# A planner's product given to either of two engines, with corrected durations: a Mamba-and-MLP block on one core

## The chip, the cores and the metric

The kernel runs on one core of a Trainium2 chip. The time is device microseconds of one execution; the figure compared is the median of several. The core's engines are TensorE (PE, matmuls, written into PSUM), VectorE (DVE), ScalarE (ACT), GpSimd (POOL) and SyncE (SP, which here issues nearly all DMAs). Each engine runs its own instructions in the order in which the program lists them, and waits at semaphores for what another engine must finish first.

## The reference, cut to what matters

The input x has 8 images of 384 channels by 1024 positions, in float32. Each image passes through a state-space ("Mamba") block with an MLP behind it and a residual; images 0 to 4 then pass through a feed-forward layer with signed weights and quantised activations.

```python
t = (t - mu) * rsqrt(var + 1e-05) * ln_w + ln_b          # norm over channels
xm, z = split(t @ in_proj_w.T, 2)                        # 768 inner channels each
xc = silu(causal_conv(xm, conv_w) + conv_b)              # 3 taps
dt, Bm, Cm = split(xc @ x_proj_w.T, [24, 40])
dt = softplus(dt @ dt_proj_w.T + dt_proj_b)
dA  = exp(dt * A)                                        # 16 states per channel
dBu = (dt * xc) * Bm
h_t = dA_t * h_(t-1) + dBu_t;  y_t = sum_n(h_t * C_t)    # scan over 1024 positions
t = ((y + xc * D) * silu(z)) @ out_proj_w.T
t = gelu(t @ mlp_w1.T + mlp_b1) @ mlp_w2.T + mlp_b2      # x = x + t
# images 0 to 4: t = t + bitlinear(gelu(bitlinear(norm(t), W1)), W2)
```

The product `dt * xc` is the one that the change's name speaks of.

## The kernel before, in words

**Stages.** Per image b there are four pieces of work. `s1` does the norm, the two input projections (PSUM tiles `p_in` and `p_z`), the convolution, the low-rank projections (`p_dbc`, `p_all`, `p_dt`), Softplus, and the product `dtx = xc * dt`. It works on two halves of 512 positions; each half has three products, each over 128 partitions by 2 x 512 elements (L817), so 48 in all. A product is written with its two inputs interleaved and then stored to DRAM (L518). `s2` is the scan: 12 units per image, 96 in all, each with four quads of states. In a unit POOL multiplies `dtx_r` by a row of B (tile `u`, L965), ACT makes `da` by Exp (L557), DVE runs the recurrences (L990), POOL or DVE multiplies by a row of C (L965, or L1010 and L1012), and PE adds the 16 states up with a folding matrix into the PSUM tile `py` (L929). `s3` does the output projection and the MLP (`p_out`, `p_h`, `p_o`, all at L541). `ffn` does the feed-forward layer (`p_y1` and `p_y2`, also L541). Most matmuls go through one helper (L541), most ACT instructions through another (L557), and evictions of PSUM through `affine` (L570 and L572 on ACT, L577 and L579 on DVE or POOL).

**The norm.** `norm` (from L590) is called 26 times. It adds three slices of 512 into `total`, in two POOL additions (L628, L629) or in one DVE reduction (L632); it takes the mean with one matmul (`p_mean`, L640), subtracts it on DVE (L643), squares on ACT, sums the squares with 12 small matmuls (`p_var`, L599), turns the result (`p_turned`, L654), adds eps (DVE, L658), raises to -0.5 (POOL, L660), spreads it with four matmuls (`p_r`, L617) and multiplies (DVE, L664).

**The planner.** No instruction stands where the Python code would put it. All operations are first written down with `add(engine, cost, emit, r=..., w=...)`: the engine, an assumed duration in us, what it reads and writes. `Plan.run` (L248) then plays them through a clock of its own: it repeatedly takes the engine that can start something first and chooses among what is ready, by rank; the scan comes before the other work. The order in which it emits is each engine's order in the program. An assumed duration therefore does not change what an instruction costs; it changes what the planner believes to be ready, and so the order of everything behind it.

Two rules of the planner matter here. The first is for operations that have a second engine (`others`). They belong to the first engine, and another may take one as a guest if it can start it at least `HOST` = 0.3 us before the first engine comes free, and would be done with it before it could start anything of its own (L329):

```python
if s + HOST < free[op.engine] and (
    first is None or s + op.others[e][0] <= first
) and (best is None or s < best[0]):
```

The second is for gaps on PE. Where the planner sees PE without work for more than `IDLE` = 0.7 us and a PSUM buffer free, it puts in `spare` matmuls of 128x256 (L451), which compute nothing that is used, one after the other until the gap is down to 0.7 us (L347). The number of `spare` matmuls in a program thus says how much standing still the planner foresaw on PE. In the profile a float32 matmul counts as two instructions.

Tiles come from rings of a few buffers; the product's output shares the ring `sq` (two buffers) with the norm's `total` and `sq`. All PSUM tiles other than `py` and `da` share the ring `mm` of three buffers, the `spare` ones too.

Of the kernel before, what the change touches and what calls it, by code (L numbers as in the profile page):

```python
# [35 lines left out]
KC = C // P  # L36
# [7 lines left out]
PER = 2  # L44
T = 512
# [26 lines left out]
MM = 0.859  # L72
# [19 lines left out]
def c_act(n):  # L92
    return 0.2 + n * 0.00084


def c_dve(n):
    return 0.17 + n * 0.00102
# [90 lines left out]
class Plan:  # L188
# [12 lines left out]
    def add(self, engine, cost, emit, r=(), w=(), claim=(), table=None, size=0, others=None,  # L201
            land=1.6, rate=350e3, lag=None, tiled=False):
        op = Op()
        op.engine, op.cost, op.emit, op.table = engine, cost, emit, table
        op.others, op.settle = others or {}, None
        op.size, op.land, op.prio = 0.03 + size / rate, land - 0.1, (*self.prio, len(self.ops))
        op.next, op.ready, op.tiles, op.tiled = [], 0.0, [], tiled
        op.lag = LAG.get(engine, 0.0) if lag is None else lag
        op.slack = SLACK if self.prio[0] < 0 else 0.0
        deps = set()  # L210

        def parts_of(t):
            t, part = t if isinstance(t, tuple) else (t, None)
            if t not in op.tiles:
                op.tiles.append(t)
                if t.ring is not None:
                    t.left += 1
            if part is None:
                if None not in t.parts:
                    t.parts[None] = [None, []]  # L220
                return list(t.parts.values())
            if part not in t.parts:
                whole = t.parts.get(None)
                t.parts[part] = [whole[0], list(whole[1])] if whole else [None, []]
            return [t.parts[part]]

        for t in claim:
            t.left += 1
            op.tiles.append(t)
        for t in r:  # L230
            for p in parts_of(t):
                if p[0] is not None:
                    deps.add(p[0])
                p[1].append(op)
        for t in w:
            for p in parts_of(t):
                if p[0] is not None:
                    deps.add(p[0])
                deps.update(p[1])
                p[0], p[1] = op, []  # L240
        deps.discard(op)
        op.wants = len(deps)
        for d in deps:
            d.next.append(op)
        self.ops.append(op)
        return op
# [144 lines left out]
class Layer:  # L391
# [198 lines left out]
    def norm(self, t, eps, scale):  # L590

        nc, add = self.nc, self.plan.add
        def columns(src, name):
            p = self.piece("mm", [P, TG], name)

            def emit():
                for k in range(KC):
                    for g in range(G):
                        nc.tensor.matmul(  # L599
                            p.real[g * DQ : (g + 1) * DQ, :], self.ones[:, :DQ],  # L600
                            src.real[:, k, g * TG : (g + 1) * TG],
                            start=(k == 0), stop=(k == KC - 1),
                        )

            add("PE", 0.79, emit, r=[src], w=[p], tiled=True)
            return p

        def spread(src, name, turned=False):
            p = self.piece("mm", [P, T], name)

            def emit():
                for g in range(G):
                    if turned:
                        by, of = src.real[:, g : g + 1], self.ident
                    else:
                        by, of = self.ident[:, g * DQ : g * DQ + 1], src.real
                    nc.tensor.matmul(  # L617
                        p.real[:, g * TG : (g + 1) * TG], by.to_broadcast([P, P]), of,
                        start=True, stop=True,
                    )  # L620

            add("PE", 0.89, emit, r=[src], w=[p])
            return p

        total = self.piece("sq", [P, T], "total")

        def in_two():
            nc.gpsimd.tensor_add(total.real, t.real[:, 0, :], t.real[:, 1, :])  # L628
            nc.gpsimd.tensor_add(total.real, total.real, t.real[:, 2, :])  # L629

        def at_once():
            nc.vector.tensor_reduce(  # L632
                total.real, t.real.rearrange("p k l -> p l k"), AX.X, ALU.add
            )

        add("POOL", 2.5, in_two, r=[t], w=[total], others={
            "DVE": (c_dve(KC * T) + 0.02, at_once)
        })
        p_mean = self.piece("mm", [P, T], "p_mean")
        add("PE", MM, lambda: nc.tensor.matmul(  # L640
            p_mean.real, self.ones, total.real, start=True, stop=True
        ), r=[total], w=[p_mean])
        add("DVE", c_dve(KC * T) + 0.05, lambda: nc.vector.scalar_tensor_tensor(  # L643
            t.real, p_mean.real.unsqueeze(1).to_broadcast([P, KC, T]), -1.0 / C, t.real,
            ALU.mult, ALU.add,
        ), r=[p_mean], w=[t])

        sq = self.piece("sq", [P, KC, T], "sq")
        self.act(lambda: sq.real, lambda: t.real, AF.Square, c_act(KC * T), r=[t], w=[sq])
        p_var = columns(sq, "p_var")  # L650
        var = self.piece("rstd", [P, TG], "var")
        self.affine(lambda: var.real, lambda: p_var.real, [p_var], [var], scale=scale, n=TG)
        p_turned = self.piece("mm", [P, G], "p_turned")
        add("PE", 0.14, lambda: nc.tensor.matmul(  # L654
            p_turned.real, var.real, self.ident[:, ::DQ], start=True, stop=True
        ), r=[var], w=[p_turned])
        rstd = self.piece("root", [P, G], "rstd")
        add("DVE", 0.15, lambda: nc.vector.tensor_scalar_add(rstd.real, p_turned.real, eps),  # L658
            r=[p_turned], w=[rstd])
        add("POOL", 1.0, lambda: nc.gpsimd.tensor_tensor(  # L660
            rstd.real, rstd.real, self.power.to_broadcast([P, G]), ALU.pow
        ), w=[rstd])
        p_r = spread(rstd, "p_r", True)
        add("DVE", c_dve(KC * T), lambda: nc.vector.tensor_mul(  # L664
            t.real, t.real, p_r.real.unsqueeze(1).to_broadcast([P, KC, T])
        ), r=[p_r], w=[t])
# [3 lines left out]
    def s1(self, b):  # L670
        nc, a, add = self.nc, self.a, self.plan.add
# [21 lines left out]
        def normed(half):  # L693
            t = self.piece(r_t, [P, KC, T], "t")
            src = a["x"][b][:, HALVES[half]].rearrange("(k p) l -> p k l", p=P)
            with self.plan.lane(14 if b == 1 else 4):
                self.load(t, lambda x: x, src, size=4 * P * KC * T)
                self.norm(t, E1 * E2, (1.0 + E2) / C)
                for k in range(KC):
                    self.affine(  # L700
                        lambda k=k: t.real[:, k, :], lambda k=k: t.real[:, k, :], [], [t[k]],
                        self.ln_b[:, k : k + 1], self.ln_w[:, k : k + 1], pool=True,
                    )
            return t
# [11 lines left out]
        for half, cols in enumerate(HALVES):  # L716
            t = normed(half)


            xc = self.split(r_x, KD, "xc")  # L720
            for m in range(KD):
                w = self.weights(r_w, KC, a["in_proj_w"][m])
# [42 lines left out]
            w = self.weights(r_w, KC, a["x_proj_w"])  # L765
# [23 lines left out]
            dt = self.split(r_x, KD, "dt")  # L789
            for k in range(0, KD, 2):  # L790
                if k % KC != 2:
                    w = self.weights(r_w, KC, a["dt_proj_w"][k // KC])
                else:
                    w, before = self.weights(r_w, KC, a["dt_proj_w"][1]), w
# [3 lines left out]
                def two(k=k, pds=pds, dbc=dbc, ws=ws):  # L798
# [8 lines left out]
                    tiled=True)  # L807
# [6 lines left out]
            d = self.dram["dtx", b]  # L814
            for p in range(KC):
                dtx = self.piece("sq", [P, T, 2], "dtx")
                add("POOL", 2.35, lambda p=p, dtx=dtx, xc=xc, dt=dt: nc.gpsimd.tensor_mul(  # L817
                    dtx.real.rearrange("p n i -> p i n"), xc.pieces[p].real, dt.pieces[p].real
                ), r=[xc[2 * p], xc[2 * p + 1], dt[2 * p], dt[2 * p + 1]], w=[dtx])
                self.store(d.real[p, :, half * L : (half + 1) * L], dtx,  # L820
                           lambda x: x.rearrange("p n i -> p (n i)"), [d[p, half]], 4 * P * L)
            d = self.dram["dt", b]
# [582 lines left out]
```

## Time and profile before

| what | value |
|---|---|
| median of 6 runs | 3201.33 us (3197.01 to 3203.86) |
| the profiled execution | 3203.86 us, of which the span from first to last instruction is 3202.0 us |
| mean granted TensorE clock | 0.987 of full speed |
| DMA | 751.78 MB, 234 GB/s of HBM traffic over the span |
| p_h, p_o, p_y1 and p_y2 matmuls (L541), busy together | 515.6 + 510.5 + 322.1 + 323.6 us |
| POOL's multiplies of the scan (L965) | 1186.3 + 900.6 + 397.1 us |
| DVE's recurrences (L990) | 870.0 + 382.0 + 281.8 us and smaller groups |

How to read it: "busy" is the time in which an engine works on an instruction; the span is the time from the first to the last instruction of the core. In the rows of groups, a line, an engine, an operation and its tiles are followed by the count, the busy time, the mean ns of one, and then the time for which the engine stood idle just before these instructions, with what ended the idle time. Tiles have the program's names without their numbers. A row of waits names who waited for whom, with the total, the number of times and the longest. Durations come from this one execution.

### The profile page before, as it was taken

To read this page: it belongs to the slowest core of one execution; us is meant where nothing else is said; L and a number is where in the kernel's file an instruction comes from. 1 tells how busy PE (TensorE), PEld (TensorE's weight loads), DVE (VectorE), ACT (ScalarE), POOL (GpSimd) and SP (SyncE) were. 2 spreads that over 40 slices of the span, in tenths; PEclk is the share of its full clock that TensorE was granted. 3 is DMA by queue.
4 is the path that set the end of the run, shared out by engine and by line. 5 is a ranking of instruction groups with operands and counts; after the bars stand their busy time and mean duration, and the time that the engine had idled before them with its cause. 6 is when DMAs were issued, how large, how long until landed. Compare 5 with 4: busy or idle time off the path is not lost.

```text
span 3202.0 us, 32487 instructions
## 1 busy us (share of the span) xinstructions
PE 3087.2 (96%) x10286; PEld 1263.8 (39%) x10286; DVE 2602.3 (81%) x2058; ACT 2020.9 (63%) x2397; POOL 2805.3 (88%) x1097
## 2 busy tenths in 40 slices
PE   9898999998999999999999999999999999999999
PEld 4333433343433443434344334343434443333333
DVE  4787887889977798798898888997788977888881
ACT  4878786767665565665675576457566565655662
POOL 2879978989989898999989999899989999998990
PEclk9899999999999999999999999999999999999999
DMA  7889878767777667766586686777767756755542
GB/s 239 295 294 302 268 233 301 258 214 246 252 277 247 206 197 247 277 224 228 197 301 243 212 299 216 250 229 271 244 222 268 243 184 215 230 183 184 170 153 72
DMA packets 348970, 751.78 MB, mean 235 GB/s; under 512 B 36480, under 2 KB 113792, under 8 KB 339584
## 3 DMA queue, kind: packets, MB, share of 16 engines
q1 hardware_dynamic: 348368, 749.61, 69.6%
q8 instruction: 83, 1.36, 0.2%
q14 instruction: 87, 0.71, 0.1%
q10 hardware_dynamic: 432, 0.09, 0.0%
HBM read 569.21 MB, written 180.36 MB: 234 GB/s over the span
## 4 chain that ended last, share of the span: by engine, by line
PE 69%; DVE 10%; DMA 8%; ACT 6%; POOL 4%; issue 3%; SPq 1%; DVEq 0%; POOLq 0%; ACTq 0%
PE p_y L541 16%; PE p_h L541 12%; PE p_o L541 11%; PE py L929 8%; PE p_z L541 6%; PE p_in L541 6%; PE p_out L541 5%; DVE da L990 3%; DVE u L990 3%; POOL u L965 3%; ACT da L557 2%; DMA dtx_r<-dtx_d 2%; ACT L557 1%; DMA dt_r<-dt_d 1%; DMA w_b<-in_mlp_w 1%
## 5 line engine op out<-in xcount | busy, mean ns | idle before, releaser
L965 POOL TENSOR_TENSOR u<-dtx_r,bc 128x2048 f32<-128x2048 f32 (+1 forms) x360 | 1186.3, 3312 | 93.6 <-PE py L929 55.0
L557 ACT ACTIVATE da<-dt_r,a_neg 128x1024 f32<-128x1024 f32 (+1 forms) x960 | 898.7, 944 | 579.1 <-DVE u L990 312.1
L965 POOL TENSOR_TENSOR u<-u,bc 128x2048 f32<-128x2048 f32 (+1 forms) x274 | 900.6, 3293 | 134.9 <-DVE u L990 122.4
L990 DVE TENSOR_TENSOR_SCAN u<-da,u 128x1024 f32<-128x1024 f32 (+1 forms) x436 | 870.0, 2007 | 155.8 <-ACT da L557 80.3
L541 PE MATMUL p_h<-t,w_b 128*128 128x512 f32 x1152 | 515.6, 600 | 15.5 <-DMA w_b<-in_mlp_w 10.2
L541 PE MATMUL p_o<-g,w 128*128 128x512 f32 x1152 | 510.5, 596 | 6.2 <-DMA w<-in_mlp_w 2.7
L990 DVE TENSOR_TENSOR_SCAN da<-da,dtx_r 128x1024 f32<-128x1024 f32 (+1 forms) x192 | 382.0, 2015 | 64.6 <-POOL dtx_r L965 43.1
L965 POOL TENSOR_TENSOR dtx_r<-dtx_r,bc 128x2048 f32<-128x2048 f32 (+1 forms) x120 | 397.1, 3314 | 1.9
L541 PEld LDWEIGHTS p_h<-t,w_b 128*128 128x128 f32 x1152 | 215.0, 191 | 307.1 <-issue 260.1
L541 PEld LDWEIGHTS p_o<-g,w 128*128 128x128 f32 x1152 | 215.1, 190 | 295.7 <-issue 279.6
L541 PE MATMUL p_y<-gf,w_n 128*128 128x512 f32 x720 | 323.6, 602 | 6.2 <-ACT dt L572 3.7
L541 PE MATMUL p_y<-tn,w_b 128*128 128x512 f32 x720 | 322.1, 602 | 6.3 <-DVE tn L664 3.5
L929 PE MATMUL py<-u,fold 128*32 128x512 f32 x2304 | 305.7, 629 | 5.9 <-POOL u L965 5.9
L990 DVE TENSOR_TENSOR_SCAN da<-da,u 128x1024 f32<-128x1024 f32 (+1 forms) x140 | 281.8, 2038 | 33.9 <-ACT da L557 18.4
L557 ACT ACT_TABLE_LOAD x211 | 270.7, 1283 | 6.5 <-DMA dt_r<-dt_d 2.8
L541 PE MATMUL p_out<-yg,w 128*128 128x512 f32 x552 | 244.9, 595 | 4.9 <-DMA w<-in_out_proj_w 2.2
L541 PE MATMUL p_in<-t,w_f 128*128 128x512 f32 x504 | 232.2, 609 | 17.4 <-ACT t L572 4.7
L541 PE MATMUL p_z<-t,w_f 128*128 128x512 f32 x504 | 233.1, 610 | 9.7 <-DMA w_f<-in_in_proj_w 8.1
L541 PEld LDWEIGHTS p_y<-gf,w_n 128*128 128x128 f32 x720 | 134.9, 191 | 190.9 <-issue 171.9
L541 PEld LDWEIGHTS p_y<-tn,w_b 128*128 128x128 f32 x720 | 135.2, 191 | 189.0 <-issue 168.6
L572 ACT ACTIVATE y<-p_y,v_vecs 128x512 f32<-128x512 f32 x145 | 98.8, 682 | 134.1 <-PE p_y L541 109.0
L572 ACT ACTIVATE g<-p_h,v_vecs 128x512 f32<-128x512 f32 x159 | 108.0, 680 | 115.4 <-PE p_h L541 114.7
(132 smaller groups left out, 3266.6 us busy)
## 6 DMA issues: line engine op xcount, KB each, us to landing
dtx_r<-dtx_d SPq DMA_DIRECT2D x72, 1024.0 KB, 5.8
dt_r<-dt_d SPq DMA_DIRECT2D x144, 512.0 KB, 5.0
w_b<-in_mlp_w SPq DMA_DIRECT2D x192, 192.0 KB, 3.3
w<-in_mlp_w SPq DMA_DIRECT2D x96, 384.0 KB, 3.3
w_f<-in_in_proj_w SPq DMA_DIRECT2D x168, 192.0 KB, 4.3
y_d<-y SPq DMA_DIRECT2D x120, 256.0 KB, 4.9
gf<-y_d SPq DMA_DIRECT2D x60, 512.0 KB, 6.7
xc_d<-xc SPq DMA_DIRECT2D x48, 512.0 KB, 6.5
```

The costliest lines, as they stand in the source:

```text
L541: self.nc.tensor.matmul(p.real, w.real[:, w0 + k, :], t.at(k0 + k), start=start and k == 0, stop=stop and k == n - 1,)
L557: lambda: self.nc.scalar.activation(out(), in_(), func, **{k: v() if callable(v) else v for k, v in kw.items()}),
L572: nc.scalar.activation(out(), in_(), AF.Identity, bias=bias, scale=scale)
L929: nc.tensor.matmul(py.real[g * DQ : (g + 1) * DQ, :], self.fold, hc, start=False, stop=(q == NQUAD - 1), skip_group_check=True,)
L965: nc.gpsimd.tensor_mul(u.real[:, x], t.real[:, x], row.real.unsqueeze(2).to_broadcast([P, n, 2]))
L990: da=da, in_u=in_u: nc.vector.tensor_tensor_scan(to(i), da.real[:, i, :], in_u(i), state.real[:, col : col + 1] if half else 0.0, ALU.mult ...
```

## The change

Four assumed durations of the norm are replaced: the 12 `p_var` matmuls 0.79 to 0.68 us, the four `p_r` matmuls 0.89 to 0.98, the `p_mean` matmul 0.859 to 0.939, the two POOL additions 2.5 to 2.64 and their single DVE form 1.757 to 1.91. The product `dtx`, so far on POOL alone, gets DVE as its second engine, with an assumed duration of 0.17 + 1024 x 0.00102 = 1.21 us; on POOL it keeps its 2.35. What is computed stays the same. Lines behind L817 move down by six.

```diff
-            add("PE", 0.79, emit, r=[src], w=[p], tiled=True)
+            add("PE", 0.68, emit, r=[src], w=[p], tiled=True)
...
-            add("PE", 0.89, emit, r=[src], w=[p])
+            add("PE", 0.98, emit, r=[src], w=[p])
...
-        add("POOL", 2.5, in_two, r=[t], w=[total], others={
-            "DVE": (c_dve(KC * T) + 0.02, at_once)
+        add("POOL", 2.64, in_two, r=[t], w=[total], others={
+            "DVE": (1.91, at_once)
         })
         p_mean = self.piece("mm", [P, T], "p_mean")
-        add("PE", MM, lambda: nc.tensor.matmul(
+        add("PE", MM + 0.08, lambda: nc.tensor.matmul(
...
-                add("POOL", 2.35, lambda p=p, dtx=dtx, xc=xc, dt=dt: nc.gpsimd.tensor_mul(
-                    dtx.real.rearrange("p n i -> p i n"), xc.pieces[p].real, dt.pieces[p].real
-                ), r=[xc[2 * p], xc[2 * p + 1], dt[2 * p], dt[2 * p + 1]], w=[dtx])
+
+                def product(engine, p=p, dtx=dtx, xc=xc, dt=dt):
+                    return lambda: engine.tensor_mul(
+                        dtx.real.rearrange("p n i -> p i n"), xc.pieces[p].real, dt.pieces[p].real
+                    )
+
+                add("POOL", 2.35, product(nc.gpsimd), w=[dtx],
+                    r=[xc[2 * p], xc[2 * p + 1], dt[2 * p], dt[2 * p + 1]],
+                    others={"DVE": (c_dve(PER * T), product(nc.vector))})
```

## The prediction, as it was made before the result

> **What bounds the kernel now.** I read the page's busy shares and chain first, then the stages, then what TensorE does while it has no work, then the rows of the instructions that the change moves.
>
> ```profile
> span 3202.0 us, 32487 instructions
> ...
> PE 3087.2 (96%) x10286; PEld 1263.8 (39%) x10286; DVE 2602.3 (81%) x2058; ACT 2020.9 (63%) x2397; POOL 2805.3 (88%) x1097
> ...
> PE 69%; DVE 10%; DMA 8%; ACT 6%; POOL 4%; issue 3%; SPq 1%; DVEq 0%; POOLq 0%; ACTq 0%
> ```
>
> TensorE is busy 96% of the span and holds 69% of the chain; POOL, with 88%, is second. But TensorE's busy time is not all work: the planner puts `spare` matmuls (L451) into gaps. Busy time by stage, first of everything, then of L451 alone (us, busy us and, in brackets, instructions of each engine; PEclk is the granted clock):
>
> ```profile
> 0.00:480.00 480.00, 437.47 (x1601) 183.70 (x1602) 354.55 (x387) 361.00 (x506) 365.81 (x245) 0.97 0.82 272
> 480.00:1280.00 800.00, 766.49 (x2568) 306.27 (x2567) 678.22 (x499) 510.43 (x574) 724.16 (x241) 0.97 0.72 244
> 1280.00:2400.00 1120.00, 1107.36 (x3670) 452.08 (x3671) 957.47 (x687) 699.21 (x758) 1047.73 (x329) 1.00 0.71 244
> 2400.00:3120.00 720.00, 698.39 (x2255) 289.09 (x2248) 596.42 (x473) 431.09 (x536) 661.72 (x282) 1.00 0.63 204
> ```
>
> ```profile
> 0.00:480.00 480.00, 26.06 (x100) 19.36 (x100) 0.97 0.82 272
> 480.00:1280.00 800.00, 4.97 (x16) 2.65 (x16) 0.97 0.72 244
> 1280.00:2400.00 1120.00, 16.05 (x66) 12.21 (x66) 1.00 0.71 244
> 2400.00:3120.00 720.00, 32.50 (x138) 25.88 (x138) 1.00 0.63 204
> ```
>
> So the span is 3007.0 us of TensorE's work (3087.2 less 80.2 of fillers), 80.2 of fillers, and 114.8 of standing still, of which 42.5 + 33.5 = 76 lie before 1280 us. The work also holds what a half-speed clock costs: a mean clock of 0.987 leaves out 0.013 x 3202 = 42 us, nearly all before 1280 us too. The work is fixed; a new plan can only change the fillers (80), the standing still (115) and the clock's loss (42).
>
> **The change part by part.** The rows that price it:
>
> ```profile
> L817 POOL TENSOR_TENSOR dtx<-xc,dt 128x1024 f32<-128x1024 f32 x48 | 113.6, 2377 | 24.8 <-ACT dt L557 17.7 <-DMA dtx_d<-dtx 6.5 <-PE p_mean L640 0.4
> L451 PE MATMUL spare<-small 128*128 128x256 f32 x322 | 80.2, 389 | 1.2 <-ACT z L570 0.8 <-DVE rstd L658 0.3
> L1012 DVE TENSOR_TENSOR dtx_r<-da,bc 128x1024 f32<-128x1024 f32 x48 | 58.5, 1219 | 2.9 <-ACT state L1004 2.1
> L628 POOL TENSOR_TENSOR total<-t 128x512 f32<-128x512 f32 x14 | 17.9, 1277 | 12.8 <-DMA t<-in_x 5.6 <-PE p_mean L640 4.2 <-PE p_var L599 1.7
> ```
>
> *Products.* In the changed program's order DVE takes 4 of the 48 products, the first of them the 30th. POOL loses 4 x 2.38 = 9.5 us. DVE has no such product now; the nearest row is L1012, the same 128x1024 multiply with the same interleaved output, at 1.22 us. The bounds are 1.2 (that row) and 2.4 (POOL's own row); I take 1.22, so DVE gains 4.9 us. DVE stands still 19% of the span, which hides it. Behind a product on DVE's queue stand scans, in three cases of four at once or after one short instruction; if Softplus is late, they wait. The product's wait for Softplus on POOL was 17.7 us in 5 times, but 16.3 of it was one wait at the start, which stays on POOL; the other four come to 1.4 us. So this wait costs 0 to about 1.4 us; I take 0.
>
> *Norm sums.* The corrected durations make the planner send 3 more of the 26 norm totals to DVE (6 instead of 3). POOL loses 3 x 2 x 1.277 = 7.7 us, DVE gains 3 x 1.91 (L632's median) = 5.7, under the same cover. In all POOL is relieved of 17.2 us of 2805 and DVE is given 10.6.
>
> *Evictions and tables.* Some 20 evictions change between ACT and DVE, and ACT has 208 table loads at L557 instead of 211 (3 x 1.28 = 3.8 us less). ACT is busy 63%; I count nothing. If ACT set the pace the loads would give at most 3.8. SP has the same 2255 issues in another order; also nothing, and no load is added.
>
> *Durations.* New values as such cost the chip nothing. They and the two moves above make the list planner choose differently from the first batches on, so that nearly every later instruction has another place. This is the part that decides.
>
> *What the new order costs TensorE.* The two programs hold the same real matmuls, and fillers: 161 before, 186 after. From the 88th of the 96 scan units to the end exactly the same real matmuls stand ahead of each unit's sums (L929; L935 after), so nothing was moved behind the last scan to pay for the fillers. Split at the units that lie at the stage borders above, fillers go from 50 to 68, 8 to 31, 33 to 13, 69 to 73 and 1 to 1. The stretch of 24 at 1312 us goes; new ones of 19, 10, 13 and 14 stand in the first third, mostly behind a norm's `p_r` or `p_turned`, where TensorE has nothing else. A filler costs 80.2/161 = 0.50 us on average and 11.04/24 = 0.46 in the long stretch; the 25 more cost 11.5 to 12.5. I take 12.
>
> **Sum.** Standing still (115) and clock loss (42) taken as unchanged: 3202.0 + 12 = 3214.0 of span, with 1.9 around it (3203.9 less 3202.0) 3215.9 for an execution like the profiled one. That one lay 2.5 above the median of 3201.3, so I predict a median of **3213.4 us**.
>
> **A rule that speaks against the change.** The trace first:
>
> ```profile
> L965 POOL TENSOR_TENSOR u<-dtx_r,bc x360: 2120/4082/4149, 85.1 to 3115.2; 128x2048 f32<-128x2048 f32 x108, 128x1024 f32<-128x1024 f32 x72
> ...
> L1010 DVE TENSOR_TENSOR dtx_r<-da,bc x144: 1196/1214/1253, 577.1 to 2769.4; 128x1024 f32<-128x1024 f32 x144
> ```
>
> These are shortest, median and longest ns. By their start times 145 of POOL's 450 long multiplies lie beside more than 1.2 us of DVE multiplies and last 4.092 us on average; the 199 with none beside them last 4.093. The Trainium skill ("SBUF — State Buffer", section "Who interferes with whom") states that a DVE instruction with two SBUF inputs contends with a GpSimd instruction that reads SBUF, and that the one that starts second is blocked until the other ends; by that rule the four products would give back 4 x 1.22 = 4.9 us of POOL's relief, and at worst the sum would be 3218. This trace disagrees: no POOL multiply exceeds 4.15 us and no DVE one at L1010 exceeds 1.27. I add nothing.
>
> **Rivals.** *No change: the fillers replace waits.* TensorE stood still 76 us before 1280 us, as between 292.3 and 297.0 us, where it had run one filler and then waited for the norm's output `t`. There the new plan has 41 more fillers (18 + 23), some 19 us; if most of that covers time that went idle anyway, which the corrected norm durations would do, the 12 us go: 3201, and 3195 to 3208 as its range. Against it: such waits are 1 to 5 us long and the added stretches mostly 4.6 to 9.
>
> *Faster: POOL sets the pace.* POOL is busy 90.5, 93.5 and 91.9% in the three middle stages, and each scan unit begins with its multiply. If its 17.2 us reach the end in full the time is 3201.3 - 17.2 = 3184. The norms can help as well:
>
> ```profile
> PE p_r L617 <- POOL rstd L660: 8.5, 5, 5.2
> ...
> PE p_var L599 <- ACT sq L557: 5.8, 4, 2.9
> ```
>
> (us in total, times, longest). It decides if the new fillers and the relief together take away over 18 us of waits and clock loss. Against it: the corrections are 0.08 to 0.15 us per instruction, while single waits here are 2.9 to 5.2; and the plan, which knows the relief, still leaves TensorE more gaps before the last scan, not fewer.
>
> *Much slower: new uncovered waits.* A redrawn order also redraws those the planner does not foresee. A wait of 3 us in the first 1280 us tends to be followed by 6.8 us at half clock, 3.4 lost: about 6.4 each. Three more of them than now, and the time is 3213 + 19 = 3232.
>
> *It does not do what it says:* 4 of 48 products is nearly nothing, so the title's edit is worth at most 9.5 us of POOL; what the forecast prices is the redrawn order.
>
> **How the numbers follow.** Forecast 0.57 (own range 3206 to 3222); fillers replace waits 0.20, 3201; POOL sets the pace 0.11, 3184; new uncovered waits 0.12, 3232. The redrawable waits and clock loss before 1280 us are 76 + about 37; a fifth of that, 22, is what I allow either side of the forecast when both ends meet. The range 3192 to 3234 leaves out most of the third case and the upper part of the fourth, under 0.2. A measurement of this kernel tells about 0.2% (6.4 us) from no change: faster means under 3194.9, slower over 3207.7. Faster: the third case and a part of the second and first, 0.14. Same: most of the second and the low end of the forecast, 0.22. Slower: 0.64.
>
> **What would show it.** L451 near x372 and 92 us; 4 products of 1.22 us on DVE and 44 on POOL (L819 there); L632 six times; TensorE's standing still near 115 us and the clock near 0.987; POOL's busy time down 17, with its share lower. In the first 480 us fillers near 34 us. If standing still falls by 12 or more, the second case holds and the step "taken as unchanged" is wrong. If POOL's idle time falls although its work did, the third case holds. If the clock falls below 0.985, the fourth.

## The result, and the profile after

| | before | changed |
|---|---|---|
| median | 3203.3 us (42 runs, 3196.3 to 3214.6) | 3192.45 us (20 runs, 3187.0 to 3199.4) |
| ratio to before | | 0.9967, 95% interval 0.9960 to 0.9975 |
| profiled execution | 3203.86 us, span 3202.0 | 3199.02 us, span 3197.2 |

The changed kernel is 0.33% faster; it was forecast 0.4% slower. Its profiled execution lies 6.6 us above its own median, so the profile shows 4.8 of the 10.9 us. One more execution of the changed kernel is on record, at 3179.8 us; it is not among the 20, and with it the median would be 3192.2 us.

The page of the changed kernel, the lines that stood first in the prediction:

```profile
span 3197.2 us, 32575 instructions
...
PE 3099.4 (97%) x10336; PEld 1274.6 (40%) x10336; DVE 2622.2 (82%) x2069; ACT 2011.2 (63%) x2392; POOL 2791.2 (87%) x1085
...
PE 74%; DVE 9%; ACT 6%; DMA 5%; issue 2%; POOL 2%; SPq 1%; DVEq 0%; ACTq 0%; POOLq 0%
```

TensorE is 12.2 us busier and the span 4.8 us shorter: it stands still 97.8 us instead of 114.8. Busy time by stage (columns as in the prediction), of everything and then of the fillers at L451:

```profile
0.00:480.00 480.00, 445.13 (x1626) 189.22 (x1626) 353.46 (x383) 362.10 (x509) 354.22 (x236) 0.98 0.82 270
480.00:1280.00 800.00, 785.28 (x2674) 320.12 (x2667) 709.00 (x524) 515.01 (x582) 736.23 (x240) 0.99 0.73 249
1280.00:2400.00 1120.00, 1101.26 (x3636) 446.39 (x3636) 953.30 (x679) 687.13 (x745) 1037.73 (x327) 0.99 0.71 242
2400.00:3120.00 720.00, 695.03 (x2234) 287.70 (x2232) 595.62 (x475) 430.64 (x538) 661.57 (x285) 0.99 0.62 202
```

```profile
0.00:480.00 480.00, 34.90 (x136) 26.72 (x136) 0.98 0.82 270
480.00:1280.00 800.00, 14.69 (x60) 10.98 (x60) 0.99 0.73 249
1280.00:2400.00 1120.00, 8.06 (x28) 5.04 (x28) 0.99 0.71 242
2400.00:3120.00 720.00, 34.32 (x146) 27.48 (x146) 0.99 0.62 202
```

Up to 1280 us the fillers rise by 18.6 us (26.06 + 4.97 to 34.90 + 14.69), as read from the order. But standing still falls by 26.4 there (76.0 to 34.9 + 14.7 = 49.6; that the fillers come to 49.6 there as well is chance), and the clock is a little higher. The 36th scan unit's last sum starts at 1287.9 us instead of 1305.7, 17.8 earlier. Later 9.5 us of waits come back between 1280 and 3120 us (12.6 + 21.6 to 18.7 + 25.0), and the last sum of the scan starts 4.8 earlier, at 3127.0.

The rows that priced the edit, in the changed kernel:

```profile
L819 POOL TENSOR_TENSOR dtx<-xc,dt 128x1024 f32<-128x1024 f32 x44 | 104.5, 2382 | 37.0 <-ACT dt L557 24.8 <-DMA dtx_d<-dtx 9.5 <-ACT da L557 1.4
L451 PE MATMUL spare<-small 128*128 128x256 f32 x372 | 92.6, 392 | 5.6 <-ACT dt L572 2.3 <-DVE t L643 1.3 <-DVE xc L736 1.3
L819 DVE TENSOR_TENSOR dtx<-xc,dt 128x1024 f32<-128x1024 f32 x4 | 11.7, 2913 | 4.0 <-PE p_var L599 4.0
```

Counts are as forecast (44 and 4 products, 186 fillers at 92.6 us). The price of a product on DVE is not: 2.91 us on average, not 1.22. The timeline around two of the four shows why (start us, us, engine, line, tiles):

```profile
1674.77 3.24 DVE L819 TENSOR_TENSOR dtx<-xc,dt 128x1024 f32<-128x1024 f32 x1
...
1932.97 3.97 DVE L819 TENSOR_TENSOR dtx<-xc,dt 128x1024 f32<-128x1024 f32 x1 [3.96 <-PE p_var L599]
...
1672.85 4.08 POOL L971 TENSOR_TENSOR u<-u,bc 128x2048 f32<-128x2048 f32 x1
1676.89 5.06 POOL L971 TENSOR_TENSOR dtx_r<-dtx_r,bc 128x2048 f32<-128x2048 f32 x1
...
1931.77 4.07 POOL L971 TENSOR_TENSOR dtx_r<-dtx_r,bc 128x2048 f32<-128x2048 f32 x1
1935.79 5.08 POOL L971 TENSOR_TENSOR u<-dtx_r,bc 128x2048 f32<-128x2048 f32 x1
```

The first of these two starts at 1674.77, beside a POOL multiply that ends at 1676.93; it ends at 1678.01, 1.08 us after that. The POOL multiply behind it takes 5.06 us instead of 4.08. So first DVE waits for POOL, and then POOL for DVE. DVE's waiting counts as busy in the profile.

### The profile page after: what moved, and what is told of

It is laid out like the page before. It is cut to its first block, busy times and chain, and to the rows that moved or that the text cites. A ratio compares the mean times of both kernels' runs of the same rounds, so it can differ in the third digit from the quotient of the medians.

```text
span 3197.2 us, 32575 instructions
## 1 busy us (share of the span) xinstructions
PE 3099.4 (97%) x10336; PEld 1274.6 (40%) x10336; DVE 2622.2 (82%) x2069; ACT 2011.2 (63%) x2392; POOL 2791.2 (87%) x1085
## 4 chain that ended last, share of the span: by engine, by line
PE 74%; DVE 9%; ACT 6%; DMA 5%; issue 2%; POOL 2%; SPq 1%; DVEq 0%; ACTq 0%; POOLq 0%
PE p_y L541 16%; PE p_h L541 14%; PE p_o L541 13%; PE py L935 9%; PE p_z L541 6%; PE p_out L541 6%; PE p_in L541 5%; DVE u L996 3%; DVE da L996 2%; ACT da L557 2%; POOL u L971 2%; ACT L557 1%; DMA w_b<-in_mlp_w 1%; PE p_dt L801 1%; DMA dtx_r<-dtx_d 1%
## 5 line engine op out<-in xcount | busy, mean ns | idle before, releaser
L971 POOL TENSOR_TENSOR u<-dtx_r,bc 128x2048 f32<-128x2048 f32 (+1 forms) x360 | 1188.7, 3317 | 114.3 <-PE py L935 79.6
L1016 DVE TENSOR_TENSOR dtx_r<-da,bc 128x1024 f32<-128x1024 f32 x144 | 171.6, 1214 | 0.3
```

Source lines behind the costliest of these rows:

```text
L971: nc.gpsimd.tensor_mul(u.real[:, x], t.real[:, x], row.real.unsqueeze(2).to_broadcast([P, n, 2]))
L1016: nc.vector.tensor_mul(u.real[:, 0, :, t], da.real[:, 0, :], cq.real)
```

## Experiments

Three theories were put to the test. *Theory 1*: the corrected durations make the planner's picture truer, and the order it gives has fewer waits. *Theory 2*: the product's second engine relieves POOL. *Theory 3*: any change of any figure draws a new order, and its time is a draw, whatever the figure means. Beside them stands the forecast's own rule, 0.48 us for each filler. Each ratio is to the kernel before, in runs on the same chip.

**e1 and e2: each half alone.** e1 takes the change without its last hunk (the product); e2 takes the last hunk alone.

> The corrected durations alone; the product stays on POOL for all 48. The program has 202 fillers (161 before, 186 after). Theory 1, truer durations give an order with fewer unforeseen waits: as fast as the changed kernel, 0.9967 of before or less, with TensorE standing still well under 115 us. Theory 2, the product's way out to DVE gives the gain: 1.000 within 0.002. Theory 3, the order is merely drawn anew: anything from 0.994 to 1.006. By the rule of the forecast (each filler 0.48 us more, the rest unchanged): 41 x 0.48 = 20 us slower, 1.006.

> The product may go to DVE, the durations stay as before. The plan gives DVE 10 of the 48 products and holds 138 fillers. Theory 1: no gain, 1.000 within 0.002 or slower. Theory 2: 10 x 2.38 us of POOL's work gone, 0.9967 or less. Theory 3: anything from 0.994 to 1.006. By the rule of the forecast: 23 fillers fewer, 11 us faster, 0.9966. In all of them the ten DVE products should take 1.8 to 4.0 us and the POOL instruction behind each should be about 1 us longer than its like, if DVE and POOL shut each other out when both read two tiles in SBUF; 1.22 us and no longer POOL instruction, if they do not.

e1: 0.9985 (0.9973 to 0.9997). e2: 1.0086 (1.0073 to 1.0099), clearly slower. So the gain that theory 2 forecast is not there, though in e2 the order changed along with the product (e3 and e5 take the two apart); the filler rule fails both times, by some 25 us in e1 and some 39 in e2, with the wrong sign in each. In e2 the trace shows 12 products on DVE (the ten of the expectation was a miscount), and the longest says most about the wait:

```profile
L819 DVE TENSOR_TENSOR dtx<-xc,dt x12: 1200/2358/8874, 140.4 to 2446.3; 128x1024 f32<-128x1024 f32 x12
```

(shortest, median, longest ns). The one of 8.87 us stood from 1825.85 through two POOL multiplies, 1825.54 to 1829.62 and 1829.57 to 1833.64: POOL began its next one while DVE was waiting.

**e3 and e5: the same orders, with the products run on POOL.** One word differs from the changed kernel (e3) and from e2 (e5):

```diff
-                    others={"DVE": (c_dve(PER * T), product(nc.vector))})
+                    others={"DVE": (c_dve(PER * T), product(nc.gpsimd))})
```

> The changed kernel's plan and order of every engine, but the four products that the plan gives to DVE run on POOL, at the place where the plan has them. It tells the product's own worth from that of the order. Theory 2: 4 x 2.38 = 9.5 us of POOL's work comes back and the gain goes: 0.9995 of before. Theories 1 and 3, the order alone gives the gain: within 0.15% of the changed kernel, 0.9955 to 0.998. With DVE and POOL shutting each other out the difference is smaller still: DVE's four products took 11.7 us instead of 4.9, and held POOL up by about 1 us each.

> The plan and order of the kernel with the product's edit alone (1.0086 of before, its DVE taking 12 products), with those products run on POOL at the same place. If the slowdown comes from DVE and POOL shutting each other out (37.5 us of DVE for 12 products instead of 14.6), it goes or mostly goes: 1.000 to 1.003. If it comes from the order, as theory 3 has it, it stays: 1.006 to 1.010. If POOL's relief was worth something, it gets slower than 1.0086.

e3: 0.9974 (0.9963 to 0.9985), beside 0.9967 for the changed kernel. e5: 1.0062 (1.0038 to 1.0085), beside 1.0086 for e2. The order keeps most of the gain in the one and most of the loss in the other. That DVE executes the products is worth less than these runs can tell.

**e4, e6 and e7: other figures.**

```diff
-DRAIN = 0.2                 # e4
+DRAIN = 0.201
...
-MODE = 0.097                # e7
+MODE = 0.098
```

e6 moves the five norm durations the wrong way:

```diff
-            add("PE", 0.79, emit, r=[src], w=[p], tiled=True)
+            add("PE", 0.90, emit, r=[src], w=[p], tiled=True)
...
-            add("PE", 0.89, emit, r=[src], w=[p])
+            add("PE", 0.80, emit, r=[src], w=[p])
...
-        add("POOL", 2.5, in_two, r=[t], w=[total], others={
-            "DVE": (c_dve(KC * T) + 0.02, at_once)
+        add("POOL", 2.36, in_two, r=[t], w=[total], others={
+            "DVE": (1.604, at_once)
...
-        add("PE", MM, lambda: nc.tensor.matmul(
+        add("PE", MM - 0.08, lambda: nc.tensor.matmul(
```

> The kernel before with one planner figure moved by a thousandth of a microsecond (what PE's drain is taken to cost, 0.200 to 0.201), which corrects nothing; the product stays on POOL. The plan is another one from the first images on: 237 fillers. Theory 3: the time moves by several us in either direction, as it does for any change. Theories 1 and 2: no gain; if it moves at all, then not below 0.998. By the rule of the forecast: 76 fillers more, 36 us slower, 1.011.

> The kernel before with the same five norm durations moved by about as much the wrong way (p_var 0.90, p_r 0.80, p_mean MM - 0.08, the additions 2.36, DVE's reduction 1.604); 158 fillers. Theory 1, truer durations give better orders: slower than before, 1.002 or more. Theory 3, the order is merely drawn anew: anything from 0.994 to 1.009, and below 1 as easily as above. By the rule of the forecast: 3 fillers fewer, 0.9996.

> The kernel before with another planner figure moved by a thousandth of a microsecond (a change of PE's mode, 0.097 to 0.098), which corrects nothing; 166 fillers. Theory 3: off by several us in either direction, 0.994 to 1.009. Theory 1: within 0.002 of before. By the rule of the forecast: 5 fillers more, 1.0007.

e4: 1.0051 (1.0038 to 1.0064). e6: 1.0020 (1.0005 to 1.0035). e7: 0.9954 (0.9937 to 0.9971), as fast as the changed kernel within the noise, from a thousandth of a microsecond that corrects nothing. This is what theory 3 says and theory 1 rules out; e1 and e6 alone would have looked like theory 1.

**e8: one input on DVE.** In the four products on DVE, dt is left out:

```diff
+                    return lambda: nc.vector.tensor_scalar(
+                        dtx.real.rearrange("p n i -> p i n"), xc.pieces[p].real, 0.01, 0.0,
+                        ALU.mult, ALU.add,
+                    )
```

> The changed kernel's order, with DVE's four products replaced by an instruction of the same output and size that reads one tile in SBUF (xc times a constant; dt is left out of these four). If two tiles read from SBUF are what makes DVE and POOL shut each other out: four instructions of about 1.2 us and no POOL multiply of 5 us behind them. If any DVE work there does it: 1.7 to 4.0 us as in the changed kernel, and POOL multiplies of 5.1 us.

3189.5 us in one run. Neither expectation held in full. The timeline at the fourth:

```profile
1925.74 3.47 DVE L824 TENSOR_SCALAR dtx<-xc 128x1024 f32<-128x1024 f32 x1 [3.95 <-PE p_var L599]
...
1924.56 4.07 POOL L977 TENSOR_TENSOR dtx_r<-dtx_r,bc 128x2048 f32<-128x2048 f32 x1
1928.60 4.54 POOL L977 TENSOR_TENSOR u<-dtx_r,bc 128x2048 f32<-128x2048 f32 x1
```

It waits for POOL too, but is done 0.58 us after POOL (1929.21 against 1928.63), and POOL's next multiply is 0.46 longer, not 1.0. All four end 0.55 to 0.58 us after a POOL instruction, where the four products of the changed kernel end 1.08 to 1.10 after one. So even the shortest of the four (1.22 us) holds a wait, the instruction's own work takes about half as long as the product's, and reading one tile is not enough to keep clear of POOL. Why it is so short, and whether a one-tile instruction at the product's pace would wait, these runs do not show. A reduction that reads one tile does keep clear: in the changed kernel POOL is busy throughout 99 of the 120 reductions at L1258, and none of the 120 takes over 0.69 us.

```profile
L1258 DVE TENSOR_REDUCE mx<-y x120: 653/660/689, 759.0 to 2533.9; 128x1 f32<-128x512 f32 x120
```

**e9 to e11: the same question on the changed kernel.** e9 moves a figure in the changed kernel, e11 the same one in the kernel before, and e10 another in the changed kernel:

```diff
-SWITCH = 0.22                # e9, e11
+SWITCH = 0.221
...
-MODE = 0.097                 # e10
+MODE = 0.096
```

> The changed kernel with one planner figure moved by a thousandth of a microsecond (a switch to the folding matmuls, 0.220 to 0.221), which corrects nothing; 180 fillers, 6 products on DVE. Theory 1, the corrected durations make orders good: within 0.002 of the changed kernel, 0.995 to 0.9985. Theory 3, each order is a draw: anything from 0.994 to 1.009, as likely over 1 as under it.

> The changed kernel with the figure for a change of PE's mode moved by a thousandth the other way (0.097 to 0.096); 216 fillers, 6 products on DVE. Theory 1: 0.995 to 0.9985. Theory 3: anything from 0.994 to 1.009. By the rule of the forecast: 30 fillers more than the changed kernel, 14 us slower than it, 1.001.

> The kernel before with the switch figure moved as in the run of that name on the changed kernel (0.220 to 0.221); 186 fillers, no product on DVE. Theory 1: not below 0.998, since the norm durations are the old ones. Theory 3: anything from 0.994 to 1.009.

e9: 0.9989 (0.9978 to 1.0000). e10: 1.0019 (1.0006 to 1.0031). e11: 1.0077 (1.0058 to 1.0097). The changed kernel's gain does not survive a redraw for certain: e10 is slower than before. In e10 the filler rule came out nearly right (1.001 forecast). Over the runs for which a figure by it was written down it had the direction right in e4, e10 and e17, and wrong in e1, e2, e6 and e7: no better than chance.

**e12: the fillers taken out.** The changed kernel's order; after the first 24 the filler emits nothing:

```diff
+        def fill():
+            fills.append(1)
+            if len(fills) <= 24:
+                self.nc.tensor.matmul(
...
+        self.plan.fill = fill
```

> The changed kernel's order with the fillers left out after the first 24 (nothing that is used is left out). If fillers hold real work up, as the forecast priced them: 162 x 0.47 = 76 us less busy time and most of that less span. If they only stand where TensorE would wait: the waits grow by about 75 us, the clock falls more often, and the time is the same or some us longer: 1.000 to 1.015 of before.

0.9966 (0.9952 to 0.9980), the changed kernel's own 0.9967. So the second expectation had the mechanism right; its range was too high, and the waits grew by less than 75 us. The page, and the busy time of the fillers by stretch:

```profile
span 3188.8 us, 31916 instructions
...
PE 3043.3 (95%) x10012; PEld 1218.2 (38%) x10012; DVE 2622.8 (82%) x2069; ACT 2011.5 (63%) x2392; POOL 2791.2 (88%) x1085
```

```profile
0.00:480.00 480.00, 11.81 (x48) 9.53 (x48) 0.95 0.81 270
480.00:3189.00 2709.00, 0.00 (x0) 0.00 (x0) 0.99 0.68 230
```

80.8 us of fillers (92.57 less 11.81) are gone. TensorE stands still 47.7 us more (145.5 against 97.8), the mean clock falls from 0.988 to 0.981 (0.978 to 0.983 in all nine executions, against 0.987 to 0.992 in those of the changed kernel), which is 0.007 x 3190 = 22 us, and the span is 8.4 us shorter than in the changed kernel's profiled execution, which lay high. So in this order a filler costs nothing: it takes the place of a wait, and of a slower clock behind the wait. This is the step that the forecast had wrong, tested by itself.

**e13 to e18: three pairs.** The same figure is moved in the kernel before and in the changed one:

```diff
-MM = 0.859                   # e13, e14
+MM = 0.860
...
-LAG = {"ACT": 0.09, "DVE": 0.08, "POOL": 0.045}     # e15, e16
+LAG = {"ACT": 0.091, "DVE": 0.08, "POOL": 0.045}
...
-SIGNAL = 0.05                # e17, e18
+SIGNAL = 0.051
```

> The kernel before with the planner's figure for a matmul moved from 0.859 to 0.860; 165 fillers. With its partner on the changed kernel it is one pair. Theory 1, the change has a worth of its own: slower than its partner by about 0.3%. Theory 3, the draw: anything from 0.994 to 1.009, and either of the two ahead.

> The changed kernel with the same figure moved, 0.859 to 0.860; 150 fillers, 9 products on DVE. Theory 1: faster than its partner by about 0.3%, and below 0.9985 of before. Theory 3: anything from 0.994 to 1.009.

> The kernel before with the figure for ACT's overlap moved from 0.090 to 0.091; 197 fillers. Second pair. Theory 1: slower than its partner by about 0.3%. Theory 3: either ahead.

> The changed kernel with the same figure moved, 0.090 to 0.091; 164 fillers, 9 products on DVE. Theory 1: faster than its partner by about 0.3%, and below 0.9985 of before. Theory 3: anything from 0.994 to 1.009.

> The kernel before with the planner's figure for a signal between engines moved from 0.050 to 0.051; 230 fillers. Third pair. Theory 1, the change has a worth of its own: slower than its partner by about 0.3%. Theory 3, the draw: either ahead. By the rule of the forecast: 101 fillers more than its partner, 48 us slower than it.

> The changed kernel with the same figure moved, 0.050 to 0.051; 129 fillers, 5 products on DVE. Theory 1: faster than its partner by about 0.3%, and below 0.9985 of before. Theory 3: anything from 0.994 to 1.009.

| pair | old durations, no choice | changed | difference |
|---|---|---|---|
| as given | 1 | 0.9967 (0.9960 to 0.9975) | -0.33% |
| `SWITCH` (e11, e9) | 1.0077 | 0.9989 | -0.88% |
| `MM` (e13, e14) | 1.0026 (1.0014 to 1.0038) | 1.0054 (1.0040 to 1.0068) | +0.28% |
| `LAG` (e15, e16) | 1.0090 (1.0077 to 1.0103) | 1.0136 (1.0123 to 1.0149) | +0.46% |
| `SIGNAL` (e17, e18) | 1.0107 (1.0089 to 1.0125) | 1.0014 (1.0001 to 1.0027) | -0.93% |

The signs are mixed, and e16 lies above the 0.994 to 1.009 that theory 3 had allowed. None of the five redraws of the changed kernel (e9, e10, e14, e16, e18) comes out below the 0.9985 that theory 1 asked for. The mean difference is -0.28% with a standard error of 0.28% (the five differences scatter by 0.63%). A lasting worth of the change is not shown, and one of a few tenths of a per cent is not excluded; that stays open.

All 16 different orders, with TensorE's account in the profiled execution (e3, e5, e8 and e12 share an order with another):

| | ratio | fillers | L451 busy, us | standing still, us | mean clock |
|---|---|---|---|---|---|
| e7 | 0.9954 | 166 | 81.8 | 100.3 | 0.990 |
| changed | 0.9967 | 186 | 92.6 | 97.8 | 0.988 |
| e1 | 0.9985 | 202 | 100.1 | 94.9 | 0.990 |
| e9 | 0.9989 | 180 | 91.3 | 93.8 | 0.988 |
| before | 1 | 161 | 80.2 | 114.8 | 0.987 |
| e18 | 1.0014 | 129 | 66.7 | 120.2 | 0.986 |
| e10 | 1.0019 | 216 | 108.0 | 103.5 | 0.989 |
| e6 | 1.0020 | 158 | 79.6 | 118.7 | 0.985 |
| e13 | 1.0026 | 165 | 82.5 | 118.7 | 0.982 |
| e4 | 1.0051 | 237 | 115.5 | 101.7 | 0.988 |
| e14 | 1.0054 | 150 | 75.3 | 134.1 | 0.983 |
| e11 | 1.0077 | 186 | 94.9 | 117.2 | 0.983 |
| e2 | 1.0086 | 138 | 71.6 | 138.2 | 0.980 |
| e15 | 1.0090 | 197 | 98.6 | 123.2 | 0.986 |
| e17 | 1.0107 | 230 | 115.7 | 109.6 | 0.986 |
| e16 | 1.0136 | 164 | 84.5 | 126.3 | 0.979 |

The ratios scatter by 0.53% (standard deviation) around 1.0036; the kernel before is the fifth fastest of its 16. The number of fillers says nothing of the time: the correlation with the ratio is 0.11. Standing still and the clock's loss (one less the mean clock, times the span) correlate with it by 0.72, and with the fillers' busy time added, by 0.95. That last figure is near an identity: what is left of the span, TensorE's work at full clock, is the same in all 16 to within 17 us. The account is of one execution each, which lies up to 10.9 us from its kernel's median (e13).

## Why the prediction was wrong, point by point

- **What bounds the kernel** held: TensorE is busy 97% with 74% of the chain, and the span is work, fillers and standing still.
- **Products, counts**: held (4 and 44). **Products, price**: wrong, 11.7 us of DVE instead of 4.9. I took L1010 and L1012 for the same kind of multiply. They read `da`, which lies in PSUM (the ring `da`, line 416), and one tile in SBUF; the product reads two tiles in SBUF. POOL's relief was smaller too: about 1 us went back for each of the four, and its busy time fell by 14.1 us (2805.3 to 2791.2) instead of 17.2. It made no measurable difference to the time (e3).
- **The rule that I set aside** was right. The Trainium skill ("SBUF — State Buffer", "Who interferes with whom") states the exclusion for a DVE instruction with two SBUF inputs against a GpSimd instruction that reads SBUF, and this trace agrees, with 5.06 instead of 4.08 us behind a product. The page also names `tensor_scalar` among those that can contend with GpSimd, when their operands meet the conditions of the two-port modes, and `tensor_reduce` among those that never do on this chip; e8 (0.46 us longer) and L1258 (0.69 us at most) agree. The kernel before had a row for it: one of the three small additions at L481, which read the same SBUF tile twice, took 1.197 us, where the next one of the same shape took 0.171, and POOL was adding beside it until 0.04 us before its end.

```profile
L481 DVE TENSOR_TENSOR join<-ident x3: 171/178/1197, 7.3 to 8.5; 128x24 f32<-128x24 f32 x2, 128x32 f32<-128x32 f32 x1
```

- **Norm sums, evictions and tables**: counts held (6 sums on DVE, 208 table loads).
- **The order**: the reading was right (25 more fillers, 92.6 us in all, 34.9 in the first stage against "near 34").
- **The failing step** is the sum's "Standing still (115) and clock loss (42) taken as unchanged". Standing still fell by 17.0 us while the fillers rose by 12.4. The clock's loss did not stay either: the 101 executions of the kernel before in the experiments have a mean clock of 0.9872, the 21 of the changed kernel 0.9895, and by the prediction's own arithmetic 0.0023 x 3200 is some 7 of the 10.9 us, an estimate that the one profiled execution (0.987 to 0.988) does not show. A filler stands where the planner foresees a wait; the wait is there with the filler or without it, and without it shows as standing still and a slower clock (e12, on the changed kernel's order). Counting the foreseen waits and holding the others fixed was no forecast at all: over the 16 orders the others run from 93.8 to 138.2 us.
- **The rivals**: "the fillers replace waits" had the right mechanism in the profile, with a chance of 0.20 and a gain that it put at nothing; its sign, standing still down by 12 or more, came true with 17.0, and the time fell below its range of 3195 to 3208. "POOL sets the pace" had nearly the right time and the wrong reason: POOL's idle time rose from 396.7 to 406.0 us, and its waits for TensorE's sums from 55.0 to 79.6. That the title's edit is worth next to nothing beside the redrawn order held in full (e3, e5).
- **The chances**: a redrawn order scatters by half a per cent here, so a forecast that gave 0.64 to "slower" on the strength of the filler count claimed a knowledge that the count does not hold.

## What to carry to other kernels

Where a list planner writes the order, a change to any of its figures is first of all a new draw: before a gain of a few tenths of a per cent is put down to the change, draw several orders around both versions, and run the same order with the edit undone. A filler that a planner puts into a foreseen gap was here a symptom of the wait and not a cost (e12); the number of fillers says little unless the unforeseen waits are known too. Before an instruction is priced by a row that looks like it, look up where each operand lies: PSUM and SBUF are two cases.

## What the runs showed of the hardware that was not expected

- DVE and POOL exclude each other for whole instructions when DVE multiplies two SBUF tiles: the product, 1.21 us with no POOL instruction beside it (e2), took up to 3.97 beside one POOL multiply in the changed kernel, up to 5.09 beside one in e2, and 8.87 there through two, and the POOL instruction behind it took about 1 us more than its like. Where the product began first (e2, 2189.59 us) it took 1.20, and the POOL multiply that began at 2189.81 took 4.92 instead of 4.08.
- POOL can begin a second multiply while DVE waits (e2, 1829.57 us), so waiting longer does not always give DVE the turn. It happened in one of e2's 12 products and in none of the changed kernel's four.
- A DVE instruction that reads one SBUF tile can wait for POOL as well (e8, all four), and a reduction of one tile did not (L1258).
- Taking out 80.8 us of TensorE's fillers (e12) left the time unchanged, although the mean clock fell from 0.988 to 0.981.
